# Queries of a transformer's attention laid out by masks from PSUM on two engines, in place of transfers

## The chip, the core and the metric

The kernel runs on one core of a Trainium2 chip. The core has five engines with a queue each: TensorE (PE; its weight loads are shown apart as PEld), VectorE (DVE), ScalarE (ACT), GpSimd (POOL) and SyncE (SP), which here only issues transfers. Each engine works through its queue in order; engines wait for one another by semaphores. Matrix products land in PSUM, from which VectorE and ScalarE bring them to the on-chip memory SBUF. The metric is the device time of one execution in microseconds (us); lower is better.

## What is computed

The program is four transformer layers in a row (L0 to L3) on `x` of 128 batches, 64 tokens and 128 channels, with a context `ctx` of the same shape and one condition vector for each batch, all in float32. Layer 0 is one cross attention; layers 1 to 3 each have a self attention, a cross attention and an MLP. There are thus seven attentions, each with 16 heads of 8 channels. Cut to one layer, with the top-16 attention that only layer 2 has:

```python
h = _ln(x) * (1 + sc_msa) + sh_msa           # scale and shift from silu(cond) @ w_ada + b_ada
qkv = h @ w_qkv + b_qkv                      # 128 -> 3 x 128
scores = einsum('bqhd,bkhd->bhqk', q, k) / sqrt(8)
o = einsum('bhqk,bkhd->bqhd', softmax(scores), v)
x = x + g_msa * (o @ w_so + b_so)
h = _ln(x) * (1 + sc_mca) + sh_mca           # cross attention: q from h, k and v from ctx
top_s, top_i = top_k(scores, 16)             # layer 2 only; elsewhere all 64 keys
x = x + g_mca * (attend(softmax(top_s), v[top_i]) @ w_co + b_co)
a, b = split(h @ w_m1 + b_m1)                # layer 2: silu(a) * b; layers 1 and 3: gelu
x = x + g_mlp * (silu(a) * b @ w_m2 + b_m2)
```

## The kernel before

The 8192 tokens are cut into 16 chunks of 8 batches (512 tokens). `chunk` writes a chunk's whole way through the four layers as a list of operations; eight lanes hold a chunk each, and a lane that is done takes the next one. So there are two waves of chunks, and 7 x 16 = 112 attentions.

The order of the work is made by a planner (class `Plan`) as the program is built. Each `op` gives an engine, an estimated cost in nanoseconds, the tiles that it writes and those that it reads. `run` chooses, again and again, the operation that can begin first by these estimates, ties going by a list of keys, and writes its instructions at the end of its engine's queue. The chip then keeps that order in each queue, whatever the real times are. `LUCK` is a list of numbers, one for each 350 choices, by which the estimated costs are shaken by up to 1%; other numbers give another order. Where the plan leaves TensorE idle for more than 1 us, it writes some matmuls of no use there (line 1229) that keep its clock up. The planner also gives out buffers: three PSUM tiles of 128x512 (`mm`), two of 128x1024 for scores (`ps`), one for outputs (`po`), 30 scratch tiles of 128x512 (`some`), three tiles for queries (`qbd`).

How an attention goes (`attention`): keys, queries and values are three products on TensorE into `mm` tiles (lines 765, 771, 789). Channels are ordered so that each group of 32 partitions holds four heads, head `j` of a group on every fourth partition from `j` on. The scores of four heads come out of one matmul (line 823, or 853 for the top-16 attention), whose query operand is `qbd`, 128 partitions x 4 heads x 512 tokens: slice `j` holds head `j`'s channels on its own partitions, and zeros on all others. Before the change it is filled like this: ScalarE copies the query out of PSUM with its bias into a scratch tile `qT` (line 774), and SyncE issues four transfers that each bring every fourth partition of it to one slice (line 778). The zeros were written once, by GpSimd (line 458), and are never written over. After the scores ScalarE takes the exponents (line 834) into `prob`, TensorE weighs the values with them (line 953), and the result goes through DRAM in four steps of transfers (lines 964, 981, 985, 990, 994) to be turned and divided by its sums (line 998), and is projected (line 1063). In the top-16 attention VectorE finds the 16 largest scores of each row (lines 891 to 906).

Around it are the layer norms: sums on VectorE (line 710), the root on GpSimd (lines 723, 724), the scaling on VectorE (line 731), a transpose on TensorE (line 698), the modulation on VectorE and GpSimd (lines 742, 743); and the MLPs (lines 1085, 1095, 1110 to 1118, 1076).

`keep_biases` (line 482) brings the biases into SBUF at the start: `bias`, and `mixed_bias` in the attention's order of channels, of which `bmix(name)` is one column.

Of the kernel before, what the change touches and what calls it, by code (L numbers as in the profile page):

```python
# [9 lines left out]
F32 = mybir.dt.float32  # L10
AF = mybir.ActivationFunctionType
ALU = mybir.AluOpType
AX = mybir.AxisListType

P = 128
B, S, D = 128, 64, 128
# [3 lines left out]
T = CB * S  # L20
# [4 lines left out]
COPIES = 8  # L25
MLP = 512
LANES = 8
NJ = MLP // P
LUCK = (
    1980, 16974, 8066, 5280, 77541, 15185, 58866, 59365, 80809, 90780, 79229,  # L30
    45879, 3353, 2761, 99804, 35781, 81655, 65576, 25895, 83999, 21415,
)
NSOME = 30
NQBD, NPROB, NVAL = 3, 8, 4
# [65 lines left out]
PE, DVE, ACT, POOL, SP, LATER = "PE", "DVE", "ACT", "POOL", "SP", "LATER"  # L100
# [31 lines left out]
class Plan:  # L132
# [42 lines left out]
        t.real, t.taken = real, True  # L175
        return t

    def op(self, engine, cost, outs, ins, give, latency=0.0, bulk=False, table=None, small=0, within=False, port=False, moves=None, rate=1.0, code=4):
        tiles = list(dict.fromkeys([*outs, *ins]))
        needs = {}  # L180
        for t in tiles:
            if t.writer is not None:
                needs[t.writer] = True
        for t in outs:
            needs.update(dict.fromkeys(t.readers))
        o = Operation(engine, cost, latency, tiles, needs, give, bulk, table, small, within, port)
        o.moves, o.rate, o.code = moves, rate, small or code
        self.count += 1
        o.serial = self.count
        o.ev = 0 if engine == PE or any(t.kind in self.PSUM for t in tiles) else 1  # L190
        for t in outs:
            t.writer, t.readers = o, []
        for t in ins:
            if t not in outs:
                t.readers.append(o)
        for t in tiles:
            t.ops.append(o)
        self.ops.append(o)
# [147 lines left out]
    def run(self, lanes, count, ahead=()):  # L346


        todo = [[] for _ in lanes] + [[(-1, o) for o in ahead]]
        chunk = 0  # L350
        while True:
            for n, write in enumerate(lanes):
                if len(todo[n]) <= self.AHEAD and chunk < count:
                    self.ops = []
                    write(chunk)
                    todo[n] += [(chunk, o) for o in self.ops]
                    chunk += 1
            best = None
            self.chosen += 1
            oldest = min((ops[0][0] for ops in todo[: len(lanes)] if ops), default=None)  # L360
            for n, ops in enumerate(todo):
                for i, (c, o) in enumerate(ops[: self.WINDOW]):
                    if o.missing or best and max(o.ready, self.engine_free[o.engine]) > best[0][0]:
                        continue
                    at = self.start(o, c in (oldest, -1) or o.within)
                    if at is None:
                        continue
                    key = at, o.ev, o.bulk, c >= 0, -(len(ops) // 40) if chunk >= count else 0, i, n
                    if best is None or key < best[0]:
                        best = key, n, i, o, at  # L370
            if best is None:
                return math.inf if any(todo) else max(self.engine_free.values())
            _, n, i, o, at = best
            del todo[n][i]
            self.give_out(o, at)
# [3 lines left out]
def kernel(ctx: ExitStack, tc: tile.TileContext, ins: dict, out: bass.AP, nchunk: int = NCHUNK):  # L379
    nc = tc.nc  # L380
    const = ctx.enter_context(tc.tile_pool(name="const", bufs=1))
# [16 lines left out]
    ident = const.tile([P, P], F32, name="ident")  # L398
# [7 lines left out]
    bias = const.tile([P, NBIAS], F32, name="bias")  # L406
    mixed_bias = const.tile([P, NBIAS], F32, name="mixed_bias")
    bm1h = const.tile([P, NJ], F32, name="bm1h")
    scT = const.tile([P, B], F32, name="scT")
    dram = ctx.enter_context(tc.tile_pool(name="dram", bufs=1, space=bass.MemoryType.DRAM))  # L410
    gates_once = [dram.tile([NCHUNK, 2, 2, NT, D], F32, name=f"once{n}") for n in range(len(GATES))]
    gates_dram = [dram.tile([NCHUNK, 2, 2 * COPIES, NT * D], F32, name=f"gates{n}") for n in range(len(GATES))]
    mods, W, plain, col, at = {}, {}, {}, {}, 0
# [15 lines left out]
    def bmix(name):  # L429
        return mixed_bias[:, col[name] : col[name] + 1]  # L430
# [6 lines left out]
    def prepare(plan, ready, pieces, all_of_it, vblocks, queries, pool, spills):  # L437
# [3 lines left out]
        op = plan.op  # L441
# [3 lines left out]
        def clear(kind, cost, give):  # L445
            t = plan.tile(lambda: None, kind)
            _, t.slot = plan.free[kind].pop()
            t.taken = True
            op(POOL, cost, [t], [], lambda: give(t.slot))
# [4 lines left out]
                nc.gpsimd.memset(v4(vblocks[k])[b * S : (b + 1) * S, :, :, 2 * HD + b : 2 * HD + b + 1], 1.0)  # L454

        for k in range(max(plan.size["qbd"], plan.size["values"])):
            if k < plan.size["qbd"]:
                clear("qbd", 1800, lambda k: nc.gpsimd.memset(queries[k], 0.0))
            if k < plan.size["values"]:
                clear("values", 1500, clear_values)  # L460
        if not all_of_it:
# [11 lines left out]
        ci, bi, th, mb, ph, biases = plan.kept(True), plan.kept(True), scratch(D), scratch(P), mm("ph"), plan.kept(True)  # L473
# [8 lines left out]
        def keep_biases():  # L482
            nc.vector.tensor_copy(bias, ph()[:, :NBIAS])
            nc.vector.tensor_copy(mixed_bias, ph()[:, P : P + NBIAS])
            at = col["L2_xcond_b_m1"]
            nc.vector.tensor_scalar(bm1h, bias[:, at : at + NJ], 0.5, None, ALU.mult)

        op(PE, 400, [ph], [bi, mb], turn_biases, code=4)
        op(DVE, 600, [biases], [ph], keep_biases)
        pieces["biases"] = [biases]  # L490
        pc = mm("pc")
        op(ACT, 320, [th], [ci], lambda: nc.scalar.activation(th(), cond_in, AF.Tanh, scale=0.5))
# [154 lines left out]
    def lane(n, plan, work, safe, acc, pieces, vblocks, queries, pool, spills):  # L647
# [6 lines left out]
        def of(*names):  # L654

            return [t for name in names for t in pieces.get(name, ())]
# [12 lines left out]
        def some(shape):  # L669


            def make():
                a = pool[t.slot]
                return a.rearrange("p (a b) -> p a b", a=shape[1]) if len(shape) == 3 else (
                    a.rearrange("p (a b c) -> p a b c", a=shape[1], b=shape[2]) if len(shape) == 4 else a
                )

            t = plan.tile(make, "some")
            return t
# [77 lines left out]
        def attention(hq, hkv, wq, bq, wk, wv, made, topk=False):  # L757
# [12 lines left out]
            pq, qbd = mm("pq"), plan.tile(lambda: queries[qbd.slot], "qbd")  # L770
            op(PE, 890, [pq, qbd, taken], [hq, *made], lambda: nc.tensor.matmul(pq(), lhsT=wq, rhs=hq(), start=True, stop=True))  # L771

            qT = some([P, T])
            op(ACT, 670, [qT, qbd], [pq, *of("biases")], lambda: nc.scalar.activation(qT(), pq(), AF.Identity, bias=bq))

            def spread():
                for j in range(4):
                    nc.sync.dma_start(out=qbd()[j::4, j, :], in_=qT()[j::4, :])

            op(SP, 2700, [qbd], [qT], spread, 1470, moves=(564, 208))  # L780


            pv = mm("pv")
            vbuf = plan.tile(lambda: vblocks[vbuf.slot], "values")
# [27 lines left out]
            def weigh(quad):  # L812


                pscs = [plan.tile(lambda: ps_s.tile([P, 2, 2, 4 * S], F32, tag="ps", name="ps"), "ps") for _ in range(2)]

                def scores():
                    for u in range(2):
                        for b in range(2):
                            for g in range(NG):  # L820
                                bb = quad * 4 + u * 2 + b
                                rows, cols = slice(32 * g, 32 * g + 32), slice(bb * S, (bb + 1) * S)
                                nc.tensor.matmul(  # L823
                                    pscs[g // 2]()[b * S : (b + 1) * S, g % 2, u].rearrange("p (h q) -> p h q", h=4),
                                    lhsT=kT()[rows, cols],
                                    rhs=qbd()[rows, :, cols],
                                    start=True,
                                    stop=True,
                                )

                prs = probs()
                op(PE, 1070, [*pscs, *prs, taken], [kT, qbd], scores, small=64, rate=0.65)
                for psc, pr in zip(pscs, prs):
                    op(ACT, 975, [pr], [psc], lambda pr=pr, psc=psc: nc.scalar.activation(  # L834
                        pr().rearrange("p g u h q -> p (g u h q)"), psc().rearrange("p g u c -> p (g u c)"),
                        AF.Exp, scale=SCALE,
                    ), table="exp")
                return prs

            def weigh_rows(i, prs):  # L840
# [18 lines left out]
                                        )  # L859

                pr = prs[gp]
                op(PE, 1088, [psc] if gp else [psc, *prs, taken], [kT, qbd], scores, small=128, within=gp > 0, rate=0.65)
                exs = []
                for half in range(2):
                    ex = some([P, 8, S])
# [260 lines left out]
        def chunk(c):  # L1126
            def qkv(w, b):
                made, w = of(w), W[w]
                return w[:, 0:D], bmix(b), w[:, D : 2 * D], w[:, 2 * D : 3 * D], made

            def q_kv(wq, bq, wkv):
                w = W[wkv]
                return W[wq], bmix(bq), w[:, 0:D], w[:, D : 2 * D], of(wq, wkv)

            x = load(x_flat, c, "x")

# [175 lines left out]
```

## Time and profile before

| | |
|---|---|
| median of 3 runs | 1788.47 us (1779.42 to 1789.54) |
| the profiled execution | 1796.32 us, of which 1794.5 us span |
| mean granted TensorE clock | 0.974 of full speed |
| ScalarE's copy of the queries, line 774 | 112, mean 694 ns |
| transfers to `qbd`, line 778 | 448 of 64 KB, median 2.5 us from issue to landing (1.7 to 6.8) |
| copies without a bias, line 767 | 112, mean 591 ns |
| copies of 128x512 on VectorE from PSUM, line 742 | 112, mean 682 ns |
| clears of `qbd`, line 458 | 3, mean 1.8 us |
| bytes moved by all transfers | 260.87 MB, mean 145 GB/s |

In the profile, busy time is the time in which an engine has an instruction running; an idle stretch is put down to what ended it (its releaser). `x<-y` names the tile written and those read. A line such as "PE ps L823 <- DMA qbd<-some: 20.6, 9, 6.0" says that TensorE at line 823 waited for the landing of a transfer to `qbd`, 20.6 us in 9 places, 6.0 at most. The rows of the 40 slices give busy tenths for slices of 44.9 us each. A table of stretches has for each: its limits and length, then busy time and count by engine, granted clock, share of the transfer engines in use, and GB/s.

### The profile page before, as it was taken

To read this page: it belongs to the slowest core of one execution; us is meant where nothing else is said; L and a number is where in the kernel's file an instruction comes from. 1 tells how busy PE (TensorE), PEld (TensorE's weight loads), DVE (VectorE), ACT (ScalarE), POOL (GpSimd) and SP (SyncE) were. 2 spreads that over 40 slices of the span, in tenths; PEclk is the share of its full clock that TensorE was granted. 3 is DMA by queue.
4 is the path that set the end of the run, shared out by engine and by line. 5 is a ranking of instruction groups with operands and counts; after the bars stand their busy time and mean duration, and the time that the engine had idled before them with its cause. 6 is when DMAs were issued, how large, how long until landed. Compare 5 with 4: busy or idle time off the path is not lost. (4 is left out here: it accounts for less than half of the span.)

```text
span 1794.5 us, 75034 instructions
## 1 busy us (share of the span) xinstructions
PE 1645.0 (92%) x30473; PEld 1146.3 (64%) x30473; DVE 1297.1 (72%) x6075; ACT 1257.5 (70%) x1830; POOL 1125.6 (63%) x1306
## 2 busy tenths in 40 slices
PE   7968999989988989999999999999999898899987
PEld 4645666656665656766666776766676666666654
DVE  8524444589999999997445359899699987896412
ACT  3745787668775766788776778778867866686652
POOL 8635565745666567686666467677776665657532
PEclk9989999989998999999999999999999998999999
DMA  7577665534433244555654466535454453455332
GB/s 209 158 217 212 189 181 150 145 98 134 131 107 109 79 139 121 160 148 158 183 162 140 141 183 181 160 105 168 145 153 118 127 160 113 123 170 141 112 111 75
DMA packets 296822, 260.87 MB, mean 145 GB/s; under 512 B 53196, under 2 KB 216212, under 8 KB 296468
## 3 DMA queue, kind: packets, MB, share of 16 engines
q1 hardware_dynamic: 296468, 255.99, 49.0%
q8 instruction: 242, 3.96, 1.0%
q14 instruction: 112, 0.92, 0.2%
HBM read 154.83 MB, written 79.04 MB: 130 GB/s over the span
## 5 line engine op out<-in xcount | busy, mean ns | idle before, releaser
L834 ACT ACTIVATE prob<-ps 128x1024 f32<-128x1024 f32 x384 | 374.4, 1023 | 96.3 <-PE ps L823 95.0
L953 PEld LDWEIGHTS po<-prob,vbuf 128*32 128x32 f32 x14336 | 216.1, 111 | 106.5 <-issue 54.1
L953 PE MATMUL po<-prob,vbuf 128*32 128x64 f32 x14336 | 256.1, 223 | 15.9 <-ACT some L963 6.5
L731 DVE TENSOR_SCALAR some<-x,parts,rstd 128x128 f32<-128x128 f32 x640 | 207.9, 387 | 55.8 <-POOL rstd L724 55.2
L823 PE MATMUL ps<-qbd,some 32*64 32x256 f32 x6144 | 227.6, 393 | 22.2 <-DMA qbd<-some 20.6
L921 POOL TENSOR_TENSOR some<-some,some 128x512 f32<-128x512 f32 x128 | 162.9, 1277 | 124.5 <-ACT some L913 75.8
L1051 POOL TENSOR_TENSOR x<-x,some 128x512 f32<-128x512 f32 x112 | 143.7, 1287 | 119.5 <-DVE some L1050 87.5
L724 POOL TENSOR_TENSOR rstd<-rstd,minus_half 128x4 f32<-128x4 f32 x192 | 199.7, 1040 | 16.0
L893 DVE MATCH_REPLACE8 some<-m,some 128x64 f32<-128x64 f32 x1024 | 206.4, 209 | 0.3 <-issue 0.3
L998 POOL TENSOR_TENSOR some<-some,some 128x512 f32<-128x512 f32 x112 | 144.5, 1292 | 94.3 <-DMA some<-spillrec 39.6
L1042 POOL TENSOR_TENSOR x<-x,some 128x512 f32<-128x512 f32 x112 | 143.1, 1281 | 55.1 <-DVE some L731 28.1
L895 DVE MAX8 m<-some 128x8 f32<-128x64 f32 x1024 | 177.0, 214 | 0.0
L891 DVE MAX8 m<-some 128x8 f32<-128x64 f32 x1024 | 172.1, 209 | 4.9 <-ACT some L871 4.8
L796 ACT COPY vbuf<-pv 64x512 f32<-64x512 f32 x224 | 153.9, 687 | 29.2 <-PE pv L789 27.2
L1050 DVE TENSOR_TENSOR some<-py,some 128x512 f32<-128x512 f32 x112 | 76.0, 683 | 133.9 <-PE py L1076 56.1
L963 ACT COPY some<-po 128x512 f32<-128x512 f32 x224 | 132.2, 590 | 57.0 <-PE po L953 42.5
L823 PEld LDWEIGHTS ps<-qbd,some 32*64 32x64 f32 x6144 | 120.1, 133 | 76.9 <-issue 34.5
L743 POOL TENSOR_TENSOR some<-some,mod_L 128x512 f32<-128x512 f32 x112 | 116.8, 1046 | 69.0 <-DVE some L742 52.0
L710 DVE BATCH_NORM_STATS2 parts<-x 128x6 f32<-128x256 f32 x320 | 119.8, 419 | 37.3 <-POOL x L1051 35.9
L698 PE MATMUL pn<-ident,some 128*128 128x128 f32 x768 | 122.8, 282 | 9.2 <-DVE some L731 2.9
L698 PEld LDWEIGHTS pn<-ident,some 128*128 128x128 f32 x768 | 89.5, 142 | 62.5 <-issue 18.8
L742 DVE TENSOR_TENSOR some<-pn,mod_L 128x512 f32<-128x512 f32 x112 | 75.7, 682 | 61.9 <-PE pn L698 46.5
(207 smaller groups left out, 3337.0 us busy)
## 6 DMA issues: line engine op xcount, KB each, us to landing
spill<-some SPq DMA_DIRECT2D x224, 256.0 KB, 3.6
some<-gates SPq DMA_DIRECT2D x224, 256.0 KB, 3.8
qbd<-some SPq DMA_DIRECT2D x448, 64.0 KB, 2.5
some<-spill SPq DMA_DIRECT2D x112, 256.0 KB, 3.6
some<-spillrec SPq DMA_DIRECT2D x112, 256.0 KB, 3.6
some<-in_ctx_dram SPq DMA_DIRECT2D x48, 256.0 KB, 5.3
gates<-once SPq DMA_DIRECT2D x7, 1024.0 KB, 9.1
x<-in_x_dram SPq DMA_DIRECT2D x16, 256.0 KB, 3.5
```

Of the source, the lines that this page charges most:

```text
L698: nc.tensor.transpose(p()[:, t * P : (t + 1) * P], x()[:, t, :], ident)
L724: nc.gpsimd.tensor_tensor(rstd(), rstd(), minus_half, ALU.pow)
L731: nc.vector.tensor_scalar(xn()[:, t, :], x()[:, t, :], mv()[:, t, 1:2], rstd()[:, t : t + 1], ALU.subtract, ALU.mult)
L796: nc.scalar.copy(v4(vbuf())[rows, :, :, 0 : 2 * HD].rearrange("p m h (d b) -> p m h d b", b=2)[:, :, :, :, b], pv()[rows].rearrange("p (m ...
L823: nc.tensor.matmul(pscs[g // 2]()[b * S : (b + 1) * S, g % 2, u].rearrange("p (h q) -> p h q", h=4), lhsT=kT()[rows, cols], rhs=qbd()[rows ...
L834: op(ACT, 975, [pr], [psc], lambda pr=pr, psc=psc: nc.scalar.activation(pr().rearrange("p g u h q -> p (g u h q)"), psc().rearrange("p g u ...
L891: nc.vector.max(m1()[:, j, :], ex()[:, j, :])
L893: nc.vector.match_replace(w()[:, j, :], m1()[:, j, :], ex()[:, j, :], GONE)
L895: nc.vector.max(m2()[:, j, :], w()[:, j, :])
L921: op(POOL, 1255, [ex], [ex, w], lambda ex=ex, w=w: nc.gpsimd.tensor_tensor(ex(), ex(), w(), ALU.mult), port=True)
L953: nc.tensor.matmul(po()[32 * j : 32 * j + 32, g, u], lhsT=vbuf()[:, at : at + 32], rhs=prs[gp]()[:, gi, u, j], start=True, stop=True,)
L998: nc.gpsimd.tensor_tensor(oT().rearrange("p (t b q) -> p b t q", b=2, q=S), oS().rearrange("p (b t q) -> p b t q", b=2, q=S), rb().rearran ...
```

## The change

`qbd` is written straight from PSUM. Slice `j` is the query plus its bias, times a mask that is 1 on head `j`'s partitions and 0 on all others, over all 128 partitions. Slices 0 and 1 are made by ScalarE, with the mask as the scale and a bias that is masked already (`bq4`); slices 2 and 3 by VectorE, which adds the bias and multiplies by the mask. The scratch tile `qT`, the four transfers and the clears of `qbd` are gone. The masks (`mask4`, from the identity matrix) and the seven masked biases are made once at the start, on VectorE. The scores now need both engines' operations (`qbd` and `qrest`); `beside` is a list of tiles that an operation writes into without waiting for their earlier writer, so that the planner may lay the two side by side. In `run`, the chunk's number becomes one of the keys by which ties are broken. The numbers of `LUCK` are others. `qkv` and `q_kv` hand on a bias's name in place of its column.

```diff
+ONACT = 2
 LUCK = (
-    1980, 16974, 8066, 5280, 77541, 15185, 58866, 59365, 80809, 90780, 79229,
-    45879, 3353, 2761, 99804, 35781, 81655, 65576, 25895, 83999, 21415,
+    89504, 74268, 44021, 21457, 23397, 22172, 36114, 67198, 95389, 4329, 84171,
+    16966, 80508, 23576, 18954, 69989, 27340, 73854, 59213, 40296, 84348,
 )
...
-        tiles = list(dict.fromkeys([*outs, *ins]))
+        tiles = list(dict.fromkeys([*outs, *ins, *beside]))
         needs = {}
         for t in tiles:
-            if t.writer is not None:
+            if t.writer is not None and t not in beside:
                 needs[t.writer] = True
...
-                    key = at, o.ev, o.bulk, c >= 0, -(len(ops) // 40) if chunk >= count else 0, i, n
+                    key = at, o.ev, o.bulk, c >= 0, -(len(ops) // 40) if chunk >= count else 0, c, i, n
...
+    mask4 = const.tile([P, 4], F32, name="mask4")
+    nc.vector.tensor_reduce(mask4, ident.rearrange("p (g j) -> p j g", j=4), AX.X, ALU.add)
+    bq4 = {b: const.tile([P, 4], F32, name=f"bq4_{b}") for b in QUERIES}
...
-            if k < plan.size["qbd"]:
-                clear("qbd", 1800, lambda k: nc.gpsimd.memset(queries[k], 0.0))
...
+            for b in QUERIES:
+                nc.vector.tensor_scalar(bq4[b], mask4, bmix(b), None, ALU.mult)
...
-            qT = some([P, T])
-            op(ACT, 670, [qT, qbd], [pq, *of("biases")], lambda: nc.scalar.activation(qT(), pq(), AF.Identity, bias=bq))
-
-            def spread():
-                for j in range(4):
-                    nc.sync.dma_start(out=qbd()[j::4, j, :], in_=qT()[j::4, :])
-
-            op(SP, 2700, [qbd], [qT], spread, 1470, moves=(564, 208))
-
+            qrest = plan.kept(True)
+
+            def heads():
+                for j in range(ONACT):
+                    nc.scalar.activation(
+                        qbd()[:, j, :], pq(), AF.Identity, scale=mask4[:, j : j + 1], bias=bq4[bq][:, j : j + 1]
+                    )
+
+            def more_heads():
+                for j in range(ONACT, 4):
+                    nc.vector.tensor_scalar(
+                        qbd()[:, j, :], pq(), bmix(bq), mask4[:, j : j + 1], ALU.add, ALU.mult
+                    )
+
+            op(ACT, 640 * ONACT, [qbd], [pq, *of("biases")], heads)
+            op(DVE, 620 * (4 - ONACT), [qrest], [pq, *of("biases")], more_heads, beside=[qbd])
...
-                op(PE, 1070, [*pscs, *prs, taken], [kT, qbd], scores, small=64, rate=0.65)
+                op(PE, 1070, [*pscs, *prs, taken], [kT, qbd, qrest], scores, small=64, rate=0.65)
```

The same `qrest` is added to what the scores of the top-16 attention read.

More of the change, by code (lines that the diff above doesn't have):

```diff
@@ L27 @@
 LANES = 8
+ONACT = 2
+QUERIES = (
+    "L0_xcond_bq", "L1_xcond_b_qkv", "L1_xcond_b_qc", "L2_xcond_b_qkv", "L2_xcond_b_q", "L3_xcond_qkv_b", "L3_xcond_q_b",
+)
 NJ = MLP // P
 LUCK = (
-    1980, 16974, 8066, 5280, 77541, 15185, 58866, 59365, 80809, 90780, 79229,
-    45879, 3353, 2761, 99804, 35781, 81655, 65576, 25895, 83999, 21415,
+    89504, 74268, 44021, 21457, 23397, 22172, 36114, 67198, 95389, 4329, 84171,
+    16966, 80508, 23576, 18954, 69989, 27340, 73854, 59213, 40296, 84348,
 )
@@ L176, in kept, with op @@
         return t
-    def op(self, engine, cost, outs, ins, give, latency=0.0, bulk=False, table=None, small=0, within=False, port=False, moves=None, rate=1.0, code=4):
-        tiles = list(dict.fromkeys([*outs, *ins]))
+    def op(self, engine, cost, outs, ins, give, latency=0.0, bulk=False, table=None, small=0, within=False, port=False, moves=None, rate=1.0, code=4, beside=()):
+        tiles = list(dict.fromkeys([*outs, *ins, *beside]))
         needs = {}
         for t in tiles:
-            if t.writer is not None:
+            if t.writer is not None and t not in beside:
                 needs[t.writer] = True
@@ L488, in prepare @@
         op(PE, 400, [ph], [bi, mb], turn_biases, code=4)
-        op(DVE, 600, [biases], [ph], keep_biases)
+        op(DVE, 1000, [biases], [ph], keep_biases)
         pieces["biases"] = [biases]
@@ L771, in attention @@
             op(PE, 890, [pq, qbd, taken], [hq, *made], lambda: nc.tensor.matmul(pq(), lhsT=wq, rhs=hq(), start=True, stop=True))
-            qT = some([P, T])
-            op(ACT, 670, [qT, qbd], [pq, *of("biases")], lambda: nc.scalar.activation(qT(), pq(), AF.Identity, bias=bq))
-            def spread():
-                for j in range(4):
-                    nc.sync.dma_start(out=qbd()[j::4, j, :], in_=qT()[j::4, :])
-            op(SP, 2700, [qbd], [qT], spread, 1470, moves=(564, 208))
+            qrest = plan.kept(True)
[8 more added lines that the diff above has]
+                        qbd()[:, j, :], pq(), bmix(bq), mask4[:, j : j + 1], ALU.add, ALU.mult
+                    )
+            op(ACT, 640 * ONACT, [qbd], [pq, *of("biases")], heads)
+            op(DVE, 620 * (4 - ONACT), [qrest], [pq, *of("biases")], more_heads, beside=[qbd])
             pv = mm("pv")
@@ L861, in weigh_rows @@
                 pr = prs[gp]
-                op(PE, 1088, [psc] if gp else [psc, *prs, taken], [kT, qbd], scores, small=128, within=gp > 0, rate=0.65)
+                op(PE, 1088, [psc] if gp else [psc, *prs, taken], [kT, qbd, qrest], scores, small=128, within=gp > 0, rate=0.65)
                 exs = []
@@ L1128, in qkv @@
                 made, w = of(w), W[w]
-                return w[:, 0:D], bmix(b), w[:, D : 2 * D], w[:, 2 * D : 3 * D], made
+                return w[:, 0:D], b, w[:, D : 2 * D], w[:, 2 * D : 3 * D], made
             def q_kv(wq, bq, wkv):
                 w = W[wkv]
-                return W[wq], bmix(bq), w[:, 0:D], w[:, D : 2 * D], of(wq, wkv)
+                return W[wq], bq, w[:, 0:D], w[:, D : 2 * D], of(wq, wkv)
             x = load(x_flat, c, "x")
```

## The prediction

> **What bounds the kernel now.** I read the page's busy totals and its 40 slices first, then the busy time in five stretches that the slices suggest, then TensorE's waits, then the timeline at its longest gaps.
>
> ```profile
> PE 1645.0 (92%) x30473; PEld 1146.3 (64%) x30473; DVE 1297.1 (72%) x6075; ACT 1257.5 (70%) x1830; POOL 1125.6 (63%) x1306
> PE   7968999989988989999999999999999898899987
> DVE  8524444589999999997445359899699987896412
> PEclk9989999989998999999999999999999998999999
> ```
>
> TensorE (PE) is busy 92% of the span, but VectorE (DVE) is at nine tenths or more in most slices from the ninth to the eighteenth and again from the twenty-fourth on: that is the top-16 selection of two waves of chunks. The stretches, with the columns PE, PEld, DVE, ACT and POOL busy:
>
> ```profile
> 0.00:403.80 403.80, 353.18 (x6639) 243.67 (x6643) 214.53 (x653) 266.54 (x363) 239.42 (x311) 0.95 0.60 173
> 403.80:807.50 403.70, 370.32 (x6906) 259.78 (x6895) 387.92 (x2245) 286.31 (x444) 267.38 (x290) 0.96 0.43 125
> 807.50:1076.70 269.20, 261.33 (x4894) 181.56 (x4892) 141.58 (x413) 203.89 (x280) 168.09 (x206) 1.00 0.55 161
> 1076.70:1615.00 538.30, 502.93 (x10027) 355.63 (x10026) 482.61 (x2628) 409.16 (x622) 364.22 (x403) 0.99 0.49 144
> 1615.00:1794.50 179.50, 157.27 (x2028) 105.62 (x2027) 70.48 (x141) 91.56 (x123) 86.44 (x99) 0.99 0.38 110
> ```
>
> So the kernel is bound by PE in the third stretch (97%), by PE and DVE together in the second (DVE 96%) and fourth (DVE 90%), and by latency in the first (PE 87%, DVE 53%) and last (PE 88%, DVE 39%). PE is idle 149.5 us in all, and the padding matmuls that the planner writes into its own idle time (line 1229) are another 67.4 us of its "busy" time, so a better order has up to 217 us to win from.
>
> What the present query path costs PE, in the list of waits and on the timeline (start, duration, instruction, idle before and its releaser):
>
> ```profile
> PE ps L823 <- DMA qbd<-some: 20.6, 9, 6.0
> PE pk L765 <- POOL some L743: 14.2, 10, 7.9
> ...
> 95.87 2.01 PE L823 MATMUL ps<-qbd,some 32*64 32x256 f32 x32 [5.46 <-DMA qbd<-some]
> 97.81 2.08 PE L1063 MATMUL py<-w_L_xcond_Wp,some 128*128 128x128 f32 x8
> ...
> 1728.48 0.69 ACT L774 ACTIVATE some<-pq,mixed_bias 128x512 f32<-128x512 f32 x1 [1.27 <-POOL x L1037]
> 1729.20 2.42 SPq L778 DMA_DIRECT2D qbd<-some  x4
> 1733.03 1.12 PE L823 MATMUL ps<-qbd,some 32*64 32x256 f32 x32 [1.34 <-DMA qbd<-some]
> ```
>
> The spread of the queries is the largest single wait of PE's matmuls. With the 0.9 us of line 853 it is 21.5 us in 12 places, 14.9 us of it before 380 us. Undisturbed, the path from ScalarE's start to the scores is 4.55 us (1728.48 to 1733.03): 0.69 copy, 2.42 to issue four transfers, the rest landing (median 2.5, at most 6.8).
>
> **The change, part by part.**
>
> *Removed per attention (112 of them):* one ScalarE copy of 0.694 us; four SP transfers, 0.588 us of SP each (2.35 us, 263 us in all); one slot of the 30 in the scratch pool. *Added:* two ScalarE copies with a scale and a bias by partition, two VectorE instructions from PSUM.
>
> ScalarE's price. Two copies with a bias back to back, lines 1110 and 1111, start at 1539.03 and end at 1540.29: 1.26 us. Copies without a bias take 591 ns (line 767), with one 694 (line 774): 103 ns for one operand by partition. If the scale operand costs as much again and nothing overlaps, the pair is 2 x 797 = 1.59 us. I take 1.4, nearer the pair that was seen; ScalarE gains 0.7 x 112 = 78 us (1257 to 1336, 74%). The Trainium skill, "ScalarE: Activation LUTs", section "What ACT_TABLE_LOAD costs", has about 93 ns for each pointer operand and an overlap of about 93 ns: by it an estimate is 1.47 us, 8 us more of ScalarE over the kernel, and no row shows an instruction with two.
>
> VectorE's price. Two instructions of 128x512 from PSUM back to back (line 742 at 26.90) take 1.28 us; singly they are 682 to 736 ns (lines 742, 1118). 112 x 1.28 = 143 us: VectorE from 1297 to 1440, 80%.
>
> *Added wait.* The scores now wait for two engines, and the PSUM tile of the query comes free with the later. On VectorE the pair stands ahead of layer norms and selection steps of other chunks; on ScalarE ahead of the exps for which PE waits. If both engines read at once the query is ready 1.4 us after PE; if one must wait for the other, 1.4 + 1.28 = 2.7. Both are shorter than 4.55, but in the second case an engine stands still, up to 1.4 us. Before, no PSUM tile is read by two engines, so no row prices this: 0 to 1.4 us each. I allow 0.35, since the engines come to the tile at different times anyway, and keep 1.4 for a rival. The rule that speaks against the change stands in the Trainium skill, "PSUM — Partial Sum Buffer", section "PSUM bank collisions raise a hardware error": two engines that read one bank in the same partitions at once collide, so software has to keep them apart. By it the reads are serial and the query takes 2.7 us; no run here shows it yet.
>
> The sum, on the profiled execution's 1796.3 us (span 1794.5 and 1.8 around it):
>
> 1. The 21.5 us of waits go, less 3 left where VectorE comes late (12 places, 0.25 each): -18.5. What is late next: at 97.81 the projection stood behind the waiting scores on PE, and it feeds the layer norm for which PE waits again at 114.51 (7.92 us, POOL line 743). That second wait moves with the first and is not shortened.
> 2. After the two long waits the rows run at half speed: 2.01 for 1.12, 2.08 for 1.16, and at 166.6 2.02 for 1.12, 2.08 for 1.13. Some 4 us: -4.
> 3. SP: 2.35 us blocks are gone from in front of the other transfers. An attention has four such steps in a row (spill, sums, reciprocals, their spread); a step meets a block with a chance of 263/1794, half a block long: 4 x 0.15 x 1.2 = 0.7 us, 80 us of chunk latency in all. PE's idle time and padding are 217 of 1794 us, 12%, so I take 12% of it: -10 (0 to -20).
> 4. In the last stretch six attentions are left, two in a row at the end; 2 x (4.55 - 2) = 5: -5. At the start three clears of 1.81 us on POOL go (they end near the first use of POOL by a layer norm at 13.52, about 1.4 us late), against eight small VectorE instructions (0.2 us by line 484; the one row of 2.3, line 486, is the first after a change of operation): -1 (-3 to +5).
> 5. VectorE in the two dense stretches. Attentions by line 774 there: 21 and 34. 21 x 1.28 = 27 us against 15.8 idle: 11 over. 34 x 1.28 = 43.5 against 55.7: it fits, at 98%, with PE at worst falling from 93.4% to the second stretch's 91.7%, 10 us. As PE does other chunks' work in a longer stretch the loss lies between +1 and +21; with the allowed waits I take +10.
> 6. ScalarE: PE and its loads wait 171 us for it in all; 6% more of it is +10 at worst; +5 (0 to 10).
> 7. The new order (other jitter numbers, older chunk first at a tie) has no instruction of its own; between -20 and +20 (a tenth of the 217 us) at the outside, most likely within 10; 0.
>
> -18.5 - 4 - 10 - 5 - 1 + 10 + 5 = -23.5, so 1772.8 on this execution. The median of the runs shown, 1788.5, lies 7.8 below the execution: **1765 us**, 1.3% faster. The terms' ends, taken as independent (below: 10, 9, 5 and 10 for terms 3, 5, 6, 7; above: 10, 6, 11, 5 and 10 for terms 3 to 7; root of the squares), give it 1747 to 1785.
>
> **Rivals.**
>
> *VectorE becomes the bound (slower).* Reads of the query's PSUM tile are serial, and the second engine stands at the head of its queue. In the dense stretches 55 attentions then take 1.28 + w of VectorE against 71.5 us of idle. With w = 1.4: 147 - 71.5 = +76, and +5 by ScalarE, against 38.5 won by 1 to 4: +42, 1831 us. It costs 1% from about w = 0.9 on (55 x 2.2 = 120, 120 - 71.5 + 5 - 38.5 = +15; +18 is 1%, at w = 0.95). For it: DVE at 96%; in-order engines; the plan's code prices the two copies as parallel. Against it: half of the time it is ScalarE that waits, and the last wait of PE in these stretches is seldom VectorE's own (the transposes of line 929 wait for POOL line 921 instead). I put this case at 1820.
>
> *No change.* The qbd waits are shown as waits only because they came last; the projections, layer norms and top-16 masks are close behind. If two thirds of terms 1 to 4 (38.5) come back as other waits, -13 + 15 (terms 5 and 6) leaves about 1790. For it: the 7.92 us wait straight after the 5.46 one. Against it: between 4.55 and 2.7 us lies more than the other waits' typical length.
>
> *A larger gain.* A shorter query path with a free SP lets eight chunks overlap better in the first stretch, where PE stands 50.6 us and DVE has room: half of that on top of the sum gives about 1740. For it: 14.9 of the 21.5 us lie there. Against it: the layer norm chain is the longer part of the same gaps.
>
> The copies replace the transfers one for one, so that it does not do what it says is no case.
>
> **How the numbers follow.** Forecast 1765, own range 1747 to 1785: 0.52. Larger gain, 1740: 0.20. No change, 1790: 0.13. VectorE the bound, 1820: 0.15. One per cent, about what a measurement of this kernel tells from none (its three runs span 10 us), puts the bounds at 1770.6 and 1806.4. Faster: the larger gain's 0.20, two thirds of the forecast (0.35) and 0.02 of the case of no change: 0.57. Same: 0.17 of the forecast and 0.11 of no change: 0.28. Slower: the slower rival's 0.15. The range of 8 in 10 cuts half of the larger gain off below and two thirds of the slower case above: 1738 to 1808.
>
> **What would show it.** No transfers to qbd; SP's 448 issues gone; wait lines of the scores for qbd's writers below 5 us in total; granted clock of 90 to 135 and 160 to 180 us nearer 1; DVE near 1440 and ACT near 1336 us busy; DVE idle in front of the new line with ScalarE's new line as releaser under 40 us in all (that is w of 0.35 x 112). It is wrong if that idle is above 100 us, if the two dense stretches grow by over 20 us, or if POOL line 743 and line 998 take up what PE no longer waits for qbd.

## The result, and the profile after

The changed kernel takes 1870.8 us in the median of 4 runs (1867.0 to 1877.8) against 1789.0 before: a ratio of 1.047, with a 95% interval of 1.044 to 1.050. It is 4.7% slower, where 1.3% faster was forecast. The profiled execution took 1874.0 us.

From the page of the changed kernel, the busy totals and two of the rows of slices (46.8 us each here):

```profile
PE 1675.3 (89%) x30501; PEld 1157.7 (62%) x30501; DVE 1429.9 (76%) x6307; ACT 1328.6 (71%) x1938; POOL 1113.7 (59%) x1303
...
PE   7888999988888889899999999899988888898997
...
DVE  7754547789989998966687488977898999985532
```

The transfers are gone and the two engines are busy about as long as was forecast (VectorE 1430 us against 1440, ScalarE 1329 against 1336). But TensorE, which was busy 92% of the span, is so for 89%, and 19 of its slices stand at nine tenths in place of 28: it is idle 196.9 us in place of 149.5. So 47 of the 78 us by which the span grew are idle time of TensorE's, and 30 are longer busy time (9 of them padding matmuls: 76.4 us in place of 67.4), at nearly the same granted clock (0.975 against 0.974). Its groups, from the list of groups (busy us, mean ns of one, then the idle time in front and what ended it), and the list of waits (us in total, times, longest):

```profile
L790 DVE TENSOR_SCALAR qbd<-pq,mixed_bias,mask 128x512 f32<-128x512 f32 x224 | 171.1, 805 | 142.2 <-ACT qbd L784 109.7 <-PE pq L778 32.3
```

```profile
DVE qbd L790 <- ACT qbd L784: 109.7, 62, 6.5
...
ACT qbd L784 <- DVE qbd L790: 57.4, 44, 3.7
```

Line 790 is VectorE's copy of the queries, line 784 ScalarE's. They write different slices and neither needs the other's result, yet each stands waiting for the other: VectorE 109.7 us in 62 of the 112 attentions, ScalarE 57.4 us in 44. The timeline shows one case of each kind (start, duration, instruction, idle before and its releaser):

```profile
97.08 1.02 PE L778 MATMUL pq<-some,w_L_xcond_W_qkv 128*128 128x512 f32 x2
...
98.14 1.53 DVE L790 TENSOR_SCALAR qbd<-pq,mixed_bias,mask 128x512 f32<-128x512 f32 x2 [1.03 <-PE pq L778]
...
99.70 1.45 ACT L784 ACTIVATE qbd<-pq,bq_L_xcond_b_qkv,mask 128x512 f32<-128x512 f32 x2 [1.83 <-DVE qbd L790]
...
1418.34 2.04 PE L778 MATMUL pq<-some,w_L_xcond_w_qkv 128*128 128x512 f32 x2
...
1420.42 1.45 ACT L784 ACTIVATE qbd<-pq,bq_L_xcond_b_qkv,mask 128x512 f32<-128x512 f32 x2 [0.80 <-PE pq L778]
...
1421.90 1.53 DVE L790 TENSOR_SCALAR qbd<-pq,mixed_bias,mask 128x512 f32<-128x512 f32 x2 [3.42 <-ACT qbd L784]
```

In both cases the one that comes first takes its pair (1.45 or 1.53 us), and the other begins 0.03 us after it ends. What they share is the PSUM tile `pq` that both read. The program holds the second reader back by a semaphore. This is the serial reading that the prediction left open and gave 0.35 us an attention. In the second case VectorE stands 3.42 us in the dense stretch, with a layer norm's scaling (line 738) and then a selection of the 16 largest behind it in its queue.

The Trainium skill, "PSUM — Partial Sum Buffer", section "PSUM bank collisions raise a hardware error", has it that software must keep two readers of a bank apart. The trace agrees as far as the program goes; no run let both read at once, so what the chip would do then is not shown here.

### The profile page after: what moved, and what is told of

It is laid out like the page before. It is cut to its first block, busy times and chain, and to the rows that moved or that the text cites. A ratio compares the mean times of both kernels' runs of the same rounds, so it can differ in the third digit from the quotient of the medians.

```text
span 1872.2 us, 74431 instructions
## 1 busy us (share of the span) xinstructions
PE 1675.3 (89%) x30501; PEld 1157.7 (62%) x30501; DVE 1429.9 (76%) x6307; ACT 1328.6 (71%) x1938; POOL 1113.7 (59%) x1303
## 5 line engine op out<-in xcount | busy, mean ns | idle before, releaser
L790 DVE TENSOR_SCALAR qbd<-pq,mixed_bias,mask 128x512 f32<-128x512 f32 x224 | 171.1, 805 | 142.2 <-ACT qbd L784 109.7
L967 PE MATMUL po<-prob,vbuf 128*32 128x64 f32 x14336 | 259.9, 223 | 14.7 <-ACT prob L848 8.0
L738 DVE TENSOR_SCALAR some<-x,parts,rstd 128x128 f32<-128x128 f32 x640 | 202.9, 380 | 35.8 <-POOL rstd L731 35.3
L705 PE MATMUL pn<-ident,some 128*128 128x128 f32 x768 | 127.6, 288 | 19.0 <-DVE some L738 6.8
```

Source lines behind the costliest of these rows:

```text
L705: nc.tensor.transpose(p()[:, t * P : (t + 1) * P], x()[:, t, :], ident)
L738: nc.vector.tensor_scalar(xn()[:, t, :], x()[:, t, :], mv()[:, t, 1:2], rstd()[:, t : t + 1], ALU.subtract, ALU.mult)
L790: nc.vector.tensor_scalar(qbd()[:, j, :], pq(), bmix(bq), mask4[:, j : j + 1], ALU.add, ALU.mult)
L967: nc.tensor.matmul(po()[32 * j : 32 * j + 32, g, u], lhsT=vbuf()[:, at : at + 32], rhs=prs[gp]()[:, gi, u, j], start=True, stop=True,)
```

## The experiments

My theory after this was *waits*: the planner lays the two pairs side by side, the chip runs them in a row, and each wait at the head of a queue makes all that is queued behind it late. The rivals were *load* (VectorE's 171 us and ScalarE's more of it are what costs) and *order* (the other jitter numbers or the tie make a worse order). "The plan's own end" below is the planner's estimate of its own order, which is no measurement; new jitter numbers were searched by it where the planner's input changed. The kernel before was run again beside the experiments, and each ratio is to the kernel before of the same set: its medians were 1787.2 us (beside the first two runs, the planned-serial one and the first with the order alone), 1783.9 (beside the row alone and the costs alone) and 1792.8 (beside the others).

**The same order with the sharing taken away.**

```diff
-                        qbd()[:, j, :], pq(), bmix(bq), mask4[:, j : j + 1], ALU.add, ALU.mult
+                        qbd()[:, j, :], ones[:, 0:1].to_broadcast([P, T]), bmix(bq), mask4[:, j : j + 1], ALU.add, ALU.mult
```

> The changed kernel with one edit: VectorE's two instructions read a constant tile in SBUF (ones, step 0) in place of the query's PSUM tile. The queries of heads 2 and 3 of each group of four are thus the mask alone. Order, counts and sizes on every engine are those of the changed kernel (1870.8 us). Waits (the two engines read the PSUM tile one after the other, and VectorE stood 109.7 us for ScalarE and ScalarE 57.4 us for VectorE): idle of each in front of the query's lines for the other falls to near 0, and the time to 1790-1825. Load (VectorE's 171 us and ScalarE's extra busy time are what costs): 1855-1875, if one such instruction still takes about 0.8 us. Order (the other jitter numbers and the tie): 1855-1875.

Measured: 1774.9 us (1769.2 to 1777.3), 95.9 less than the changed kernel and 0.9913 of the kernel before (0.988 to 0.994); below the range expected for *waits*. This run and the next leave the true queries of two slices out, so they show times only. From its page and its list of groups:

```profile
PE 1642.3 (93%) x30501; PEld 1140.4 (64%) x30501; DVE 1439.3 (81%) x6307; ACT 1326.6 (75%) x1938; POOL 1137.1 (64%) x1303
```

```profile
L790 DVE TENSOR_SCALAR qbd<-ones,mixed_bias,mask 128x512 f32<-128x512 f32 x224 | 171.7, 807 | 3.8 <-PE ps L837 3.8
```

Counts are equal on every engine, and VectorE's copies happen to take the same (171.7 us, mean 807 ns, against 171.1 and 805). Only the idle time in front of them has gone, from 142.2 to 3.8 us. So load and order are not what made the changed kernel slower than the one before: with both in place it is faster. Both engines still write to one tile `qbd` here, so it is the reading of `pq`, not the writing of one tile, that makes them take turns. The edit also removes VectorE's 32.3 us of waiting for the product itself; the runs on what the planner knows, below, keep that need and give back most of the time all the same.

TensorE's part shows how a wait elsewhere is paid. Its 30501 instructions are the same, but its idle time falls from 196.9 to 133.1 us, and its busy time from 1675.3 to 1642.3, as the granted clock goes from 0.975 to 0.988. Two thirds of the 97 us of span are idle time, a third is longer busy time; the clocks alone would make some 22 of those 33 us (an estimate: 1642.3 x 0.988 / 0.975 gives 1664.2), and the rest was not traced. And the loss is not in the dense stretches alone. From the view of the tile `pq`, the first and last product of three of the seven attentions, in the changed kernel:

```profile
L778 PE MATMUL pq<-some,w_L_xcond_W_qkv x32: 592/592/697, 97.1 to 1323.6; 128*128 128x512 f32 x32
...
L778 PE MATMUL pq<-some,w_L_xcond_qkv_w x32: 592/592/697, 473.7 to 1760.6; 128*128 128x512 f32 x32
...
L778 PE MATMUL pq<-some,w_L_xcond_q_w x32: 592/592/1223, 534.0 to 1810.1; 128*128 128x512 f32 x32
```

and with the other data:

```profile
L778 PE MATMUL pq<-some,w_L_xcond_W_qkv x32: 592/592/697, 90.3 to 1254.9; 128*128 128x512 f32 x32
...
L778 PE MATMUL pq<-some,w_L_xcond_qkv_w x32: 592/592/697, 447.2 to 1667.2; 128*128 128x512 f32 x32
...
L778 PE MATMUL pq<-some,w_L_xcond_q_w x32: 592/592/697, 503.2 to 1714.3; 128*128 128x512 f32 x32
```

The queues are the same, so the same product can be compared: it is 6.8 us late at 97 us, 26.5 at 474, 30.8 at 534, 68.7 at 1324, 93.4 at 1761, 95.8 at 1810. That is 5 to 8% of the time gone by at each of them: it grows where VectorE has room as well as where it has none.

**The same order without VectorE's copies.** Slices 2 and 3 are filled once at the start, and the loop over them is left out of `more_heads`.

```diff
             def more_heads():
-                for j in range(ONACT, 4):
...
+                pass
...
+                nc.gpsimd.memset(q[:, ONACT:4, :], 1.0)
                 queries.append(q)
```

> The changed kernel with VectorE's part of the queries left out: slices 2 and 3 are filled once with ones at the start (3 clears of 128x1024 on GpSimd), and VectorE writes nothing for each attention. The plan, and with it the order of all else, is the changed kernel's. Waits: as the run with other data within 15 us, since VectorE has room once nothing stands still. Load: clearly faster than the run with other data, 1790-1820 against 1855-1875. Order: still 1850-1875.

Measured: 1748.3 us (1747.9 to 1750.2), 26.7 below the run with other data. "Within 15 us" was too little: VectorE's 172 us of copies do cost something, about a sixth of their length, but less than a third of what the sharing costs.

**What the planner knows.** Only what the planner is told differs; the instructions are the changed kernel's but for what the planner adds itself (30465 matmuls in place of 30501, 1936 instructions on ScalarE in place of 1938).

```diff
-            op(ACT, 640 * ONACT, [qbd], [pq, *of("biases")], heads)
-            op(DVE, 620 * (4 - ONACT), [qrest], [pq, *of("biases")], more_heads, beside=[qbd])
+            op(ACT, 725 * ONACT, [qbd], [pq, *of("biases")], heads)
+            op(DVE, 765 * (4 - ONACT), [qrest], [pq, qbd, *of("biases")], more_heads)
```

> The changed kernel with the planner told how it is: VectorE's operation needs ScalarE's (planned behind it, not beside it), costs of 2 x 725 and 2 x 765 ns as the profile has them, and jitter numbers searched anew for these costs (the plan's own end 1822.6 us against 1812.5 of the changed kernel's). Instructions are the same. Waits that come of a plan that lays side by side what runs in a row: VectorE's idle time for ScalarE in front of the query's line falls from 109.7 to under 40 us, and the time to 1805-1840. Load: 1850-1880, as VectorE and ScalarE have the same to do. Order alone: anything, as the order is new; the waits in front of the line tell.

Measured: 1790.7 us (1785.2 to 1797.8), 80 less than the changed kernel and below the range expected, a ratio of 1.002 to the kernel before (1.000 to 1.004). From its list of waits:

```profile
DVE qbd L790 <- ACT qbd L784: 68.6, 32, 9.3
...
ACT qbd L784 <- PE pq L778: 41.2, 45, 5.0
```

VectorE still waits 68.6 us for ScalarE, more than the 40 expected, but in 32 places in place of 62 one behind the other as in the plan, and ScalarE no longer waits for VectorE at this line. TensorE's matmuls wait 6.3 us in all for the two query lines, where they wait 45.7 us in the changed kernel (the sum of the waits that name line 784 or 790). So the waiting costs far less where the plan has it: by the ratios to the kernel before, this run is 1.1% above the run with other data and the changed kernel 5.6% (the orders are not the same). As this run had new numbers too, three more take it apart.

> The changed kernel with other jitter numbers, searched anew for the same plan (the plan's own end 1810.4 us against 1812.5; the order differs from the fourth number on, some 1050 of 7350 choices in). Both copies are still planned side by side. Waits: 1855-1890, with VectorE's idle time for ScalarE in front of the query's line again above 85 us; the planned-serial run owes its 1790.7 us to what the plan knew. Order (the changed kernel's numbers were merely bad on the chip): 1790-1830.

Measured: 1871.7 us (1868.7 to 1878.0), with VectorE 107.1 us idle for ScalarE. Another order of the same plan is as slow as the first: the first numbers were not bad luck.

The two halves of what was told, each alone and with numbers searched anew to nearly the same plan's own end:

```diff
-            op(DVE, 620 * (4 - ONACT), [qrest], [pq, *of("biases")], more_heads, beside=[qbd])
+            op(DVE, 620 * (4 - ONACT), [qrest], [pq, qbd, *of("biases")], more_heads)
```

> The planner is told only that VectorE's copies come behind ScalarE's; the costs are the changed kernel's (2 x 640 and 2 x 620 ns, too low by 0.17 and 0.29 us a pair). Numbers searched anew (the plan's own end 1809.6 us). If the side-by-side plan is what costs: 1785-1815. If the low costs are: 1850 or more.

```diff
-            op(ACT, 640 * ONACT, [qbd], [pq, *of("biases")], heads)
-            op(DVE, 620 * (4 - ONACT), [qrest], [pq, *of("biases")], more_heads, beside=[qbd])
+            op(ACT, 725 * ONACT, [qbd], [pq, *of("biases")], heads)
+            op(DVE, 765 * (4 - ONACT), [qrest], [pq, *of("biases")], more_heads, beside=[qbd])
```

> The planner is told only the costs (2 x 725 and 2 x 765 ns); the two pairs are still planned side by side. Numbers searched anew (the plan's own end 1809.5 us). If the side-by-side plan is what costs: 1850-1885, VectorE idle for ScalarE in front of the query's line above 85 us. If the low costs are: 1785-1815.

Measured: with the row alone 1795.7 us (1794.1 to 1796.7; ratio 1.007, 1.005 to 1.009), with the costs alone 1846.4 us (1844.0 to 1849.2; ratio 1.035, 1.032 to 1.037). From the list of waits with the row alone (ScalarE does not wait for VectorE at this line there), then with the costs alone:

```profile
DVE qbd L790 <- ACT qbd L784: 71.0, 43, 8.9
...
DVE qbd L790 <- ACT qbd L784: 99.6, 59, 9.5
...
ACT qbd L784 <- DVE qbd L790: 50.9, 42, 4.7
```

The row gives back 75 us and the costs 24, a little more than the range allowed them. So the changed kernel loses its time because two copies that run in a row are planned side by side; costs that are too low add to it.

**One engine reads the tile.** All four slices by ScalarE (`ONACT = 4`, cost 4 x 715), then all four by VectorE from a copy in SBUF:

```diff
+            qT = some([P, T])
+            op(ACT, 690, [qT], [pq, *of("biases")], lambda: nc.scalar.activation(qT(), pq(), AF.Identity, bias=bmix(bq)))
...
             def heads():
...
+                for j in range(4):
+                    nc.vector.tensor_scalar(qbd()[:, j, :], qT(), mask4[:, j : j + 1], None, ALU.mult)
...
+            op(DVE, 1680, [qbd], [qT], heads, port=True)
```

> All four slices by ScalarE, none by VectorE, so one engine reads the tile; cost 4 x 715 ns, numbers searched anew (the plan's own end 1865.1 us). Waits: no wait of one engine for the other is left, so the time follows ScalarE's load: some 112 x 1.4 = 157 us more of ScalarE than in the changed kernel (1329 to 1485 us busy) and 171 us less of VectorE; the time about 10 to 20 us below the plan's end, 1835-1860, faster than the changed kernel's 1870.8 though the plan says it is 53 us slower. Load (ScalarE's exps feed PE, so ScalarE's load costs more than VectorE's): 1870-1920.

> ScalarE copies the queries with their bias out of PSUM once, as before, and VectorE makes all four slices from that copy in SBUF (4 instructions, planned at 1680 ns), numbers searched anew (the plan's own end 1814.7 us). One engine reads the PSUM tile, and VectorE's need of ScalarE is in the plan. Waits: 1785-1825, with little idle time that the plan did not lay out. Load: VectorE is to do as much as in the changed kernel or more (4 x 0.45 = 1.8 us an attention against 1.53), so 1850 or more.

Measured: 1824.8 us (1823.0 to 1827.7) and 1809.0 us (1808.1 to 1810.3). Both are faster than the changed kernel, though the plan put the first 53 us behind it and the second level with it. All by ScalarE came out below the range expected. Both are slower than the kernel before (ratios 1.019 and 1.010). That the copies by masks are more work for an engine than one copy and four transfers would explain it, but no run shows that this is the reason.

**The order by itself.** The kernel before, with the tie by chunk and new numbers, twice:

> The kernel before with the other two parts of the change alone: the chunk's number as a key for ties, and other jitter numbers, here searched anew (the plan's own end 1772.7 us against 1803.1 of the kernel before). Transfers to the queries as before. Order (the tie or the numbers cost time by themselves): 1810 or more. Waits or load: 1760-1800, no slower than before by over 1%.

> The kernel before with the tie by chunk and a second set of searched numbers (the plan's own end 1812.3 us, against 1772.7 of the first reordered run and 1803.1 of the kernel before). If a plan that matches the chip carries over, the time moves with the plan's end: 1790-1810, about 30-40 us above the first reordered run. If the tie itself is what made that one fast: below 1775.

Measured: 1765.9 us (1758.9 to 1766.3; ratio 0.986, 0.983 to 0.989) and 1789.9 us (1785.0 to 1798.5; ratio 1.000, 0.997 to 1.002). The first is the fastest run here that computes all of the function, and beats both kernels. The same tie with other numbers gives no gain, so it is the order that the numbers found; what the tie does alone was not tried. Set beside the plans' own ends:

| run | plan's own end | median measured | difference |
|---|---|---|---|
| before | 1803.1 | 1789.0 | -14 |
| before, reordered, first and second | 1772.7, 1812.3 | 1765.9, 1789.9 | -7, -22 |
| planned serial; row only | 1822.6; 1809.6 | 1790.7; 1795.7 | -32; -14 |
| all by ScalarE; from SBUF | 1865.1; 1814.7 | 1824.8; 1809.0 | -40; -6 |
| changed; other numbers; costs only | 1812.5; 1810.4; 1809.5 | 1870.8; 1871.7; 1846.4 | +58; +61; +37 |

Every plan in which no two engines are laid side by side on one PSUM tile ends 6 to 40 us before its estimate on the chip; each of the three that do lay them so ends 37 to 61 us after it.

## Why the prediction was wrong

*The step that failed* is the allowance in the added wait: "I allow 0.35, since the engines come to the tile at different times anyway", 39 us for 112 attentions. Measured it is 109.7 / 112 = 0.98 us of VectorE and 57.4 / 112 = 0.51 of ScalarE. Coming at different times doesn't help an engine whose queue was laid out as if it could begin at once. Against these 167 us of waiting stand the 95.9 us that went with the sharing. The prediction's own sign of being wrong, over 100 us of VectorE's idle time for ScalarE, came true.

*The slower rival* had the right mechanism: serial reads, an engine that stands at the head of its queue, and the point near w = 0.9 us of VectorE's waiting in an attention from which it costs 1%. It got 0.15, and its price of +42 at the very most is half of the +82 measured, and the runs show two things that it left out. It let the wait cost something only in the dense stretches, against VectorE's idle time there; the lag grows from the start, outside them too. And it counted the waits of VectorE's queue alone; ScalarE's 57.4 us and TensorE's 45.7 us behind both came on top, and the clock stayed at 0.975 where the run with other data has 0.988. What each adds was not separated.

*Term 1* (the waits for the queries go) was right in size where the plan is right: 6.3 us of TensorE's waits are left in the planned-serial run, of 21.5. But TensorE's idle time as a whole did not fall there: it is 151.9 us (1785.9 of span less 1634.0 busy), against 149.5 before. In the changed kernel the term failed: the scores' matmuls alone wait 23.8 us for the two lines, where under 5 was the sign of being right.

*Term 2* (clock after the long waits) held where it was looked for (0.98 from 93.6 to 187.2 us, against 0.88 before), but the clock fell elsewhere, and its mean came out at 0.975 against 0.974.

*Prices:* ScalarE's pair is 1.45 us against 1.4 taken. The estimate of 1.47 by the Trainium skill's page "ScalarE: Activation LUTs", section "What ACT_TABLE_LOAD costs", was nearer. VectorE's pair is 1.53 against 1.28, one instruction 803 ns in the median against the 682 of the row it was taken from, which has no operand by partition: 28 us too little load. That VectorE's total came out at 1430 all the same is chance: 112 x 1.53 = 171 us on the 1297 of before would be 1468, and why the rest shows 38 us less was not traced.

*Term 5*, even as load alone, was too low: taking VectorE's copies away altogether gave 26.7 us, where +10 with a bound of +21 was forecast.

*Term 4's* start went the way forecast: the first scores begin at 25.54 us in place of 27.95, 2.4 us sooner where 1 was forecast. The term's reading of line 486 (2.3 us, "the first after a change of operation") does not hold: in the changed kernel three rows in a row of one operation (line 491) take 0.9 to 1.1 us there, and end together at 7.8 us.

*Terms 3 and 6* were not separated by any run. *Term 7*, the order, was bounded at 20 us either way; the kernel before moved by -23 and +1 with other orders.

*The case of no change* is what becomes of this design when it is planned as it runs: 1790.7 and 1795.7 us. As that case has it, what is won at the scores comes back as other waits (TensorE's 151.9 us of idle time, above). Whether the copies' load or the 68.6 us of planned waiting brings them back was not separated.

## What to carry to other kernels

Where the order of the work is fixed ahead, an idle stretch that the plan holds can cost far less than one that comes as a surprise and is passed on in every queue that hangs on it. Here 69 and 71 us of planned waiting left the kernel, in other orders, 1.1 and 1.6% above the run with other data, and 167 us of unplanned waiting 5.6%. Before two engines are given one buffer, find out whether they are let at it together, and plan it as it is. Price a wait over the whole span, not only where its engine looks full. And when a change brings a new order with it, run the old design with a new order and the new design with another one: here order alone was worth up to 23 us, against 96 of the mechanism.

## What the runs showed of the hardware

A VectorE instruction of 128x512 with a bias and a mask by partition takes 789 to 815 ns from PSUM, in 224 instances. The same from a constant column in SBUF takes 448 to 1555 ns, with a median of 542 and nearly the same mean (807 against 805); with one operand by partition from a full SBUF tile it is 389 to 1580, median 480. So an SBUF source is faster at its best and far less steady. In that last run GpSimd's line 1004 was also seen to wait 34.9 us for VectorE's copies; what makes the long ones long was not tested.

No wait of TensorE's matmuls in the changed kernel is longer than 3.4 us, where the falls of the clock that the prediction read followed waits of 5.5 and 6.0. Yet the same instructions took 33 us more busy time than with the other data, at a granted clock of 0.975 against 0.988. The falls do not need a long wait: from 169.1 to 172.5 us TensorE was at full clock and busy 2.12 of 3.4 us, with one wait of 1.28 us (for VectorE's line 738), and from 172.5 to 175.9 the granted clock was 0.51. At 1417.60 a wait of 1.42 us stands before a stretch (1418.4 to 1421.8) at 0.50: that is the pair of products that takes 2.04 us in the second case of the timeline of the first section, and 1.02 in the first case. What else decides about a fall was not traced.
